# The first stage's step behind the next sequence's value product, in two groups of heads

## The chip, the cores and the metric

The kernel runs on one core of one Trainium2 chip. The metric is the time of one execution on the device in microseconds (us); the time before is the median of 3 runs, 1147.43 us.

## The reference

The input x has 8 sequences of 512 tokens with 512 features, in float32. Each token is normalized; the normalized x goes into two branches, whose product is added to x:

```python
xn = _layernorm(x, axis=-1)
s = _L0_attn_ref(xn, Wq, Wk, Wv, Wo, Wg1, Wg2, norm_weight)
g = _silu(_L0_ffn_ref(xn, gate_w, Wg, Wu, Wd, sWg, sWu, sWd, shared_gate_w))
x = x + s * g
```

The first branch is attention with a decay, without softmax, in 16 heads of 32 features, computed in chunks of 128 tokens with a state that is carried from chunk to chunk:

```python
q = rotate(silu(x @ Wq)); k = rotate(silu(x @ Wk)); v = x @ Wv
scores = einsum('bthd,bshd->bhts', qi, ki) * D          # D: decay, causal
o_intra = einsum('bhts,bshd->bthd', scores, vi)
o_inter = einsum('bthd,bhde->bthe', qi * decay_q, S)
S = lam_C * S + einsum('bshd,bshe->bhde', ki * decay_k, vi)
o = group_rmsnorm(o * sigmoid(x @ Wg1 @ Wg2)) * weight
return o @ Wo
```

The second branch is a mixture of experts: a router picks 4 of 16 experts for each token, each expert is a gated two-layer network with 128 hidden features, and a shared expert with its own gate is added:

```python
probs = softmax(flat @ gate_w.T); weights, chosen = top_k(probs, 4)
out_e = (silu(flat @ Wg[e]) * (flat @ Wu[e])) @ Wd[e]
mixed = sum of weights (normalized) * out_e;  return mixed + shared * sigmoid(flat @ shared_gate_w)
```

## The kernel before

The program is written out from Python, without a loop on the device. Engines are PE (matmuls), DVE and ACT (vector work; both also read the results of PE out of PSUM), POOL, and SP, which issues most DMAs. Each engine works its own queue in order. A wait for a tile, or for a buffer that a new tile takes over, stops the engine at that instruction and all that is queued behind it. A recording layer puts each engine's instructions in an order; those of PE are held in the order of the text (`on_pe`, L211 on, ties each group to the one before), and the others follow from it.

The stages, in order of time:

- The first stage, written as the generator `first()`, goes over all 8 sequences. For each it normalizes x (`norm`), transposes it on PE (`turn`, L277 on: 16 transposes into PSUM tiles psT, L289, copied by ACT into xT, L291, stored by SP, L297), computes the router's logits (`route_1`: plT, L306; `route_2`: pl, L318, from which DVE makes lg, L320; `route_3`: DVE picks the four experts and makes the tile mask, L331 to L345), and the shared expert (`share_1`: pg and pu, L355; `share_2`: pys, L371, four products, copied by ACT into sh, L374, stored by SP, L375). Its pieces end at the `yield`s.
- Attention of sequence 0 runs beside the end of the first stage: `along()` takes, on average, 9 pieces of `first()` for every 5 of its calls. It is handed to `sequence(0, ...)` as `step`.
- `sort()`, also a generator, takes the masks of all sequences and works out where each token stands in the lists of the experts: ptotal and pbefore on PE (L387), copied by ACT (L388), then a chain on DVE and POOL (L393 to L468), and the routing weights wt (exp on ACT, L470; products on POOL, L471 and L475; den on DVE, L473 and L474).
- Attention of sequence 1, with the building of the lists (`table`, DVE and ACT, products pn, L565) between its matmuls; the experts' weights (wexp) are loaded meanwhile.
- The block stage: rows are gathered by expert (L1153, POOL) and go through the experts.
- Attention of sequences 2 to 7, each with the mixture of the experts' outputs beside it.

In `sequence(b, step, ...)` the 16 heads are taken in 4 groups of 4 (g = 0 to 3). For each group: `scores` (state products into pk, L714; the scores ps, L725, in four PSUM tiles, one for each head; DVE multiplies each with the decay into sc, L750), a `step`, then for g = 0 and 1 the key product of group g + 2 (`key`, pk, L659), and for g = 2 and 3 the value product of the next sequence, `value(n, 0)` and `value(n, 2)` (pv, L615, four matmuls of 512 columns, which the profile shows as 8; ACT copies pv into v, L619). Then `by_token` (L691), a second step, the query product or `value(n, 1)`, `output` (po, L766 and L772; on, L776), and a third step. Behind the four groups come `value(n, 3)`, `squares` (sq on ACT, L783; pr on PE, L786), `inverse` (L790, L794) and the first key and query products of the next sequence.

PSUM has eight banks: seven are given out by `bank(tag)`, four of tag "a" (ps, psT, plT, pl, two of the four pys, ptotal, pbefore, pr and others), one "m" (pk of `key`, pg, even pv, the third pys), two "d" (pq, pu, odd pv, the first pys, po), and one "k". A new tile takes the bank of its tag that the recording layer expects free first, and waits for the last reader of the tile before it.

Which pieces the two edited steps take in sequence 0: in the third group (g = 2) the one piece `turn(7)`; in the fourth (g = 3) `route_2(7)` and `share_2(7)`.

Of the kernel before, what the change touches and what calls it, by code (L numbers as in the profile page):

```python
# [22 lines left out]
G, HG = 4, 4  # L23
# [74 lines left out]
def tile_block(ctx: ExitStack, tc: tile.TileContext, a: dict, out: bass.AP):  # L98
# [8 lines left out]
    def bank(tag, name):  # L107
        return pp.tile([P, 512], F32, tag=tag, name=name, bufs={"a": 4, "k": 1, "m": 1, "d": 2}[tag])
# [101 lines left out]
    @contextmanager  # L210
    def on_pe():  # L211

        with tc.issue_after(last_pe[-1]) if last_pe else nullcontext():
            yield
        traced = nc.cur_bb.bb.instructions
        last_pe.append(next(
            i for i in reversed(traced) if i.engine == mybir.EngineType.PE))
# [377 lines left out]
    def load_xT(b, pool=None):  # L595
        xT = (pool or home(b)).tile([P, KC, N], F32, tag="xT", name=f"xT_{b}", bufs=1)
        nc.sync.dma_start(xT.rearrange("p k n -> p (k n)"), xT_d[b])
        xT_of[b] = xT
# [10 lines left out]
    def value(b, t):  # L609
        if t == 0:  # L610
            v_of[b] = att.tile([P, NC, D], F32, tag="v", name=f"v_{b}", bufs=2)
        pv = bank("d" if t % 2 else "m", f"pv_{b}_{t}")
        for k in range(KC):
            with on_pe():
                nc.tensor.matmul(  # L615
                    pv, lhsT=xT_of[b][:, k, t * P : (t + 1) * P], rhs=wv[:, k, :],
                    start=(k == 0), stop=(k == KC - 1))
            between[0]()
        nc.scalar.copy(v_of[b][:, t, :], pv)  # L619
# [4 lines left out]
    def gate_1(b):  # L624
        pg1 = bank("a", f"pg1_{b}")
        with on_pe():
            for k in range(KC):
                for t in range(NC):
                    nc.tensor.matmul(
                        pg1[t * Q : (t + 1) * Q, :P], lhsT=wg1[:, k, :],  # L630
                        rhs=xT_of[b][:, k, t * P : (t + 1) * P],
                        start=(k == 0), stop=(k == KC - 1))
        g1_of[b] = att.tile([P, P], F32, tag="tmp", name=f"g1_{b}", bufs=TMP)
        nc.scalar.copy(g1_of[b], pg1[:, :P])

    def gate_2(b, tiles=range(NC), banks="aaaa"):
        if 0 in tiles:
            on_of[b] = home(b).tile([P, G, N], F32, tag="on", name=f"on_{b}", bufs=1)
        g1 = g1_of[b]
        p2s = {t: bank(banks[t], f"p2_{b}_{t}") for t in tiles}  # L640
        with on_pe():
            for g in range(G):
                for t in tiles:
                    tq = slice(t * Q, (t + 1) * Q)
                    nc.tensor.matmul(
                        p2s[t][:, g * P : (g + 1) * P], lhsT=wg2[tq, g * P : (g + 1) * P],
                        rhs=g1[tq, :], start=True, stop=True)
        for t in tiles:
            nc.scalar.activation(
                on_of[b][:, :, t * P : (t + 1) * P],  # L650
                p2s[t].rearrange("p (g n) -> p g n", n=P), AF.Sigmoid)
        if NC - 1 in tiles:
            g1_of.pop(b)
# [24 lines left out]
    def key(b, g, ps=None):  # L678
        kT_of[g] = rotated(b, g, "k", wk, ps)

    def query(b, g):
        qT_of[g] = rotated(b, g, "q", wq)

    def by_token(b, g):

        if not kept:
            kept.append(bank("k", f"pk_{b}_{g}"))
        pk = kept[0]
        with on_pe():
            for c in range(NC - 1):  # L690
                nc.tensor.transpose(  # L691
                    pk[:, c * P : (c + 1) * P], kT_of[g][:, c * C : (c + 1) * C], ident)
        kd = scr[0].tile([P, NC - 1, HG, HD], F32, tag="kd", name=f"kd_{b}_{g}")
        by_chunk = pk[:, : (NC - 1) * P].rearrange("p (c h d) -> p c h d", c=NC - 1, d=HD)
        for j in range(HG):
            nc.scalar.activation(
                kd[:, :, j, :], by_chunk[:, :, j, :], AF.Copy,
                scale=dk[:, g * HG + j : g * HG + j + 1])
        kd_of[g] = pk[:, (NC - 1) * P :], kd
# [55 lines left out]
    def output(b, g):  # L755
        po = bank("d", f"po_{b}_{g}")
        st, qd, sc = st_of.pop(g), qd_of.pop(g), sc_of.pop(g)
        with on_pe():
            for c in range(1, NC):
                if carry:  # L760
                    nc.tensor.matmul(  # L761
                        po[:, c * C : (c + 1) * C], lhsT=st[:, c - 1, :], rhs=qd[:, c - 1, :],
                        start=(c == 1), stop=False)
                for j in range(0 if carry else HG):
                    hs = slice(j * HD, (j + 1) * HD)
                    nc.tensor.matmul(  # L766
                        po[hs, c * C : (c + 1) * C], lhsT=st[hs, c - 1, :], rhs=qd[hs, c - 1, :],
                        start=(c == 1), stop=False)
            for c in range(NC):
                for j in range(HG):  # L770
                    h = g * HG + j
                    nc.tensor.matmul(  # L772
                        po[j * HD : (j + 1) * HD, c * C : (c + 1) * C],
                        lhsT=v_of[b][:, c, h * HD : (h + 1) * HD],
                        rhs=sc[j][:, c], start=False, stop=(c == NC - 1))
        nc.vector.tensor_tensor(on_of[b][:, g, :], po, on_of[b][:, g, :], ALU.mult)  # L776
# [16 lines left out]
    def inverse(b):  # L793
        nc.vector.reciprocal(rs_of[b], rs_of[b])  # L794
# [18 lines left out]
    def project(b, t):  # L813
        pw = bank("d", f"pw_{b}_{t}")
        with on_pe():
            for g in range(G):
                nc.tensor.matmul(  # L817
                    pw, lhsT=on_of[b][:, g, t * P : (t + 1) * P], rhs=wo[:, g, :],
                    start=(g == 0), stop=(g == G - 1))
        return pw  # L820
# [36 lines left out]
    def sequence(b, step, projected, before=None, defer=False, also=lambda: None):  # L857


        n = b + 1  # L860

        def project_tiles(q, ts):
            if q is not None:
                for t in ts:
                    projected(q, t, project(q, t))


        fill = ([0], [1], [2], [3], [], [], [], [])
        for g in range(G):
            scores(b, g)  # L870
            step()
            if g + 2 < G:
                key(b, g + 2)
            else:
                value(n, 2 * (g - 2))
            if g + 1 < G:
                by_token(b, g + 1)
            project_tiles(before, fill[2 * g])
            step()
            if g + 2 < G:  # L880
                query(b, g + 2)
                if g + 3 == G and n not in xT_of:
                    load_xT(n)
            if g + 2 == G:
                value(n, 1)
            if g == 0 and b not in on_of:
                gate_2(b)
            project_tiles(before, fill[2 * g + 1])
            if fill[2 * g + 1] == [NC - 1]:
                on_of.pop(before, None)  # L890
            output(b, g)
            if defer and g + 2 == G:
                gate_1(n)
            step()
        v_of.pop(b)
        if n == FIRST:
            for _ in range(4):
                next(filling)
            gate_1(n)
            next(filling, None)  # L900
            for e in range(E - LATE // 2, E):
                nc.sync.dma_start(wexp[:, e, :], a["experts"][:, e, :])
            squares(b)
            inverse(b)
            value(n, 3)
            normed(b)
            experts_of_blocks()
            return
        if defer:
            gate_2(n)  # L910
        value(n, 3)
        also()
        squares(b)
        step()
        inverse(b)
        key(n, 0)
        also()
        query(n, 0)
        normed(b)
        also()  # L920
        if not defer:
            step()
        key(n, 1)
        by_token(n, 0)
        if defer:
            step()
        query(n, 1)
        also()
        if not defer:
            gate_1(n)  # L930
            project_tiles(b, [0, 1])
            also()
            project_tiles(b, [2, 3])
            also()
            on_of.pop(b)
        step()
# [156 lines left out]
    along()  # L1093
    enter(0, along)
    sequence(0, along, spill, also=lambda: next(sorting, None))
    for _ in sorting:
        pass
# [373 lines left out]
```

## Time and profile before

| | |
|---|---|
| runs | 1147.18, 1147.43, 1147.70 us; median 1147.43 |
| the profiled execution | 1147.87 us, its span 1146.0 us |
| mean granted clock of PE | 0.997 |
| busy over the span | PE 1114.3 us (97%), DVE 753.2 (66%), POOL 444.8 (39%), ACT 428.8 (37%) |
| scores of sequence 0's third group (ps, L725) | start at 153.13 us |
| scores of sequence 0's fourth group | start at 178.51 us |
| sorting starts on PE (ptotal, L387) | 188.79 us |
| first gather of the block stage (L1153) | 286.98 us |

PE is the bound almost everywhere: what counts is where it idles. Times in a timeline are counted from the start of the span. A row merges instructions of one kind that follow each other; `x16` is their number, and the bracket at the end has how long the engine idled before and what it waited for. "issue" means that nothing the profile shows held it. Busy times of PE include a modelled end of each matmul, so the length of a block is better read from the start of one row to the start of the next.

### The profile page before, as it was taken

To read this page: it belongs to the slowest core of one execution; us is meant where nothing else is said; L and a number is where in the kernel's file an instruction comes from. 1 tells how busy PE (TensorE), PEld (TensorE's weight loads), DVE (VectorE), ACT (ScalarE), POOL (GpSimd) and SP (SyncE) were. 2 spreads that over 40 slices of the span, in tenths; PEclk is the share of its full clock that TensorE was granted. 3 is DMA by queue.
4 is the path that set the end of the run, shared out by engine and by line. 5 is a ranking of instruction groups with operands and counts; after the bars stand their busy time and mean duration, and the time that the engine had idled before them with its cause. 6 is when DMAs were issued, how large, how long until landed. Compare 5 with 4: busy or idle time off the path is not lost. (4 is left out here: it accounts for less than half of the span.)

```text
span 1146.0 us, 21657 instructions
## 1 busy us (share of the span) xinstructions
PE 1114.3 (97%) x7838; PEld 685.4 (60%) x7838; DVE 753.2 (66%) x1608; ACT 428.8 (37%) x924; POOL 444.8 (39%) x430
## 2 busy tenths in 40 slices
PE   7999999999999999999999999999999999999998
PEld 4445554455567777777777885555645545546453
DVE  6358744998345454454555666868789497797774
ACT  3223424254353333333333442252442522522541
POOL 4213100200323333333332314835868848858111
PEclk9999999999999999999999999999999999999999
DMA  9995431191789999999999976714747528544012
GB/s 342 317 316 192 155 133 47 47 383 46 234 184 234 252 237 237 241 235 235 233 235 273 251 192 251 264 49 147 233 125 250 165 86 256 149 129 139 20 38 74
DMA packets 163932, 218.50 MB, mean 191 GB/s; under 512 B 89840, under 2 KB 99184, under 8 KB 161776
## 3 DMA queue, kind: packets, MB, share of 16 engines
q1 hardware_dynamic: 142704, 146.76, 41.5%
q0 software_dynamic: 21120, 70.34, 23.5%
q8 instruction: 64, 1.05, 0.4%
q14 instruction: 44, 0.36, 0.1%
HBM read 126.78 MB, written 72.43 MB: 174 GB/s over the span
## 5 line engine op out<-in xcount | busy, mean ns | idle before, releaser
L1222 PE MATMUL pgu<-xts,wst 128*128 128x256 f32 x896 | 202.6, 379 | 0.0
L1222 PEld LDWEIGHTS pgu<-xts,wst 128*128 128x128 f32 x896 | 170.1, 190 | 46.2 <-issue 19.9
L1321 POOL DMA_INDIRECT yg<-y_d,place x128 | 140.1, 1095 | 30.7 <-issue 19.7
L1153 POOL DMA_INDIRECT more<-xn_d,slot x69 | 65.5, 950 | 218.9 <-DVE w L1206 107.2
L1237 PE MATMUL py<-wexp,slb 128*128 x272 | 130.0, 594 | 1.5 <-DVE slb L1229 1.5
L1241 DVE TENSOR_SCALAR y<-py,w 128x512 f32<-128x512 f32 x136 | 101.9, 751 | 42.7 <-PE py L1237 23.7
L615 PE MATMUL pv<-wv,xT 128*128 128x512 f32 x256 | 118.6, 604 | 1.3 <-ACT sh L374 1.0
L659 PE MATMUL pk<-xT,wk 128*128 128x512 f32 x256 | 118.1, 603 | 0.0
L659 PE MATMUL pq<-xT,wq 128*128 128x512 f32 x256 | 115.7, 593 | 0.4 <-PEq L1285 0.4
L1228 ACT ACTIVATE slb<-pgu 128x256 f32<-128x256 f32 (+1 forms) x80 | 28.1, 351 | 214.7 <-PE pgu L1222 163.0
L1153 POOL DMA_INDIRECT xg<-xn_d,slot x67 | 63.8, 952 | 104.7 <-DVE w L1206 36.7
L817 PE MATMUL pw<-wo,on 128*128 128x512 f32 x224 | 100.5, 595 | 3.8 <-DVE m L1359 3.1
L1363 POOL TENSOR_TENSOR xo<-xo,m 128x512 f32<-128x512 f32 x31 | 45.3, 1460 | 142.1 <-DVE m L1359 134.8
L1229 DVE TENSOR_TENSOR slb<-slb,pgu 128x256 f32<-128x256 f32 (+1 forms) x80 | 30.5, 381 | 104.7 <-ACT slb L1228 60.1
L1204 DVE COPY wst<-wexp 128x512 f32 x160 | 61.3, 424 | 43.3 <-DVE y L1241 18.3
L1186 ACT COPY xts<-pl 128x512 uint16<-128x512 uint16 x110 | 84.4, 770 | 2.2 <-DMA pl<-xg 1.7
L750 DVE TENSOR_TENSOR sc<-ps,dmask 128x512 f32<-128x512 f32 x128 | 79.1, 678 | 3.6 <-remote 1.9
L659 PEld LDWEIGHTS pq<-xT,wq 128*128 128x128 f32 x256 | 47.2, 190 | 54.2 <-issue 53.3
L615 PEld LDWEIGHTS pv<-wv,xT 128*128 128x128 f32 x256 | 46.2, 191 | 52.1 <-issue 47.6
L659 PEld LDWEIGHTS pk<-xT,wk 128*128 128x128 f32 x256 | 46.2, 189 | 50.7 <-issue 48.3
L817 PEld LDWEIGHTS pw<-wo,on 128*128 128x128 f32 x224 | 41.3, 190 | 52.9 <-issue 45.2
L1237 PEld LDWEIGHTS py<-wexp,slb 128*128 128x128 f32 x272 | 45.4, 191 | 29.2 <-issue 26.8
(193 smaller groups left out, 1724.9 us busy)
## 6 DMA issues: line engine op xcount, KB each, us to landing
y_d<-y SPq DMA_DIRECT2D x136, 256.0 KB
wexp<-in_experts SPq DMA_DIRECT2D x16, 768.0 KB
sh_d<-sh SPq DMA_DIRECT2D x32, 256.0 KB
xT<-xT_d SPq DMA_DIRECT2D x8, 1024.0 KB
m<-sh_d SPq DMA_DIRECT2D x32, 256.0 KB
xo<-in_x SPq DMA_DIRECT2D x32, 256.0 KB
out<-xo SPq DMA_DIRECT2D x31, 256.0 KB
x<-in_x SPq DMA_DIRECT2D x7, 1024.0 KB
```

The costliest lines, as they stand in the source:

```text
L615: nc.tensor.matmul(pv, lhsT=xT_of[b][:, k, t * P : (t + 1) * P], rhs=wv[:, k, :], start=(k == 0), stop=(k == KC - 1))
L659: nc.tensor.matmul(ps, lhsT=w[:, k, g * P : (g + 1) * P], rhs=xT_of[b][:, k, :], start=(k == 0), stop=(k == KC - 1))
L750: masked[:] = [nc.vector.tensor_tensor(s, pss[j].rearrange("p (c t) -> p c t", t=C), dmask[:, g * HG + j].unsqueeze(1).to_broadcast([P, NC ...
L817: nc.tensor.matmul(pw, lhsT=on_of[b][:, g, t * P : (t + 1) * P], rhs=wo[:, g, :], start=(g == 0), stop=(g == G - 1))
L1153: nc.gpsimd.indirect_dma_start(out=row(i), out_offset=None, in_=xn_d, in_offset=bass.IndirectOffsetOnAxis(ap=slot[:, i : i + 1], axis=0))
L1186: (nc.vector.tensor_copy if j in by_dve else nc.scalar.copy)(xt[:, u, KP:, :].bitcast(U16).rearrange("p k (t h) -> p h k t", h=2), pls[j % ...
L1204: nc.vector.tensor_copy(to, wflat[:, bass.ds(off + u * KC * F, KC * F)])
L1222: nc.tensor.matmul(pg[:, o * n * P : (o + 1) * n * P], lhsT=wst[j % 2][k // KP][:, (k % KP * 2 + o) * F :][:, :F], rhs=xt[:, :, k, :], sta ...
L1237: nc.tensor.matmul(py, lhsT=hT[:, u * P : (u + 1) * P], rhs=wflat[:, bass.ds(off + KC * 2 * F, D)], start=True, stop=True)
L1241: gone.append(nc.vector.tensor_scalar(y, py, w[:, u : u + 1], None, ALU.mult).ins)
L1321: nc.gpsimd.indirect_dma_start(out=yg, out_offset=None, in_=y_d, in_offset=bass.IndirectOffsetOnAxis(ap=place[:, r, g : g + 1], axis=0))
L1363: nc.gpsimd.tensor_tensor(xo, xo, m, ALU.add)
```

## The change

In sequence 0 (`b == 0`), for the third and fourth group (`g + 2 >= G`), the first of the three steps of a group is taken behind the value product of sequence 1 and no longer between the scores and that product. Everything else, the other sequences and groups too, is as it was. Lines below the edit are 4 further down.

```diff
         for g in range(G):
             scores(b, g)
-            step()
+            late_step = b == 0 and g + 2 >= G
+            if not late_step:
+                step()
             if g + 2 < G:
                 key(b, g + 2)
             else:
                 value(n, 2 * (g - 2))
+            if late_step:
+                step()
             if g + 1 < G:
                 by_token(b, g + 1)
             project_tiles(before, fill[2 * g])
```

## The prediction

> **What bounds the kernel now.** I first read the page: PE is busy 97% of the span, so time is won only where PE stands still or stops coming back late. The chain of waits holds no piece between 140 and 330 us (asked for that window, it answers 0 pieces), so the edited place, sequence 0, had to be read elsewhere. Second, the waits of PE between 150 and 195 us (columns: instruction, line, what it waited for; us, times, longest):
>
> ```profile
> PE psT L289 <- DVE sc L750: 1.0, 1, 1.0
> PE pv L615 <- ACT sh L374: 1.0, 1, 1.0
> PE pl L318 <- DVE sc L750: 0.8, 1, 0.8
> ```
>
> These are all that PE waits for there, and each stands at one of the two edited places. Third, the timeline there (start us, us, engine, line, operation, tiles):
>
> ```profile
> 153.13 1.17 PE L725 MATMUL ps<-qT,kT 32*128 32x128 f32 x32
> 154.61 2.48 DVE L750 TENSOR_TENSOR sc<-ps,dmask 128x512 f32<-128x512 f32 x4
> 155.35 2.43 PE L289 MATMUL psT<-ident,x 128*128 128x128 f32 x16 [1.04 <-DVE sc L750]
> 157.61 3.60 PE L615 MATMUL pv<-wv,xT 128*128 128x512 f32 x8
> ...
> 178.51 1.17 PE L725 MATMUL ps<-qT,kT 32*128 32x128 f32 x32
> 179.70 2.49 DVE L750 TENSOR_TENSOR sc<-ps,dmask 128x512 f32<-128x512 f32 x4
> 180.44 0.33 PE L318 MATMUL pl<-ident,lT 128*128 128x128 f32 x1 [0.77 <-DVE sc L750]
> 180.61 3.60 PE L371 MATMUL pys<-sw,h 128*128 128x512 f32 x8
> 182.10 0.22 DVE L320 COPY lg<-pl 128x68 f32<-128x68 f32 x1
> 183.20 1.28 ACT L477 ACT_TABLE_LOAD   x1
> 184.53 0.48 DVE L345 TENSOR_TENSOR mask<-mask,oh 128x64 f32<-128x64 f32 x2
> 185.25 3.70 PE L615 MATMUL pv<-wv,xT 128*128 128x512 f32 x8 [1.04 <-ACT sh L374]
> 186.99 0.63 ACT L470 ACTIVATE wt<-wt 128x512 f32<-128x512 f32 x1
> 188.79 1.02 PE L387 MATMUL ptotal<-mask,ones 128*128 128x512 f32 x2
> ```
>
> The scores of a group fill all four banks of tag "a"; DVE empties them one by one in 2.48 us, and the step behind them (psT in the third group, pl and pys in the fourth) wants just those banks. In the fourth group the value product then wants the bank of tag "m" that pys has filled and that ACT empties late, behind a table load. Fourth, what follows:
>
> ```profile
> 201.00:228.00 27.00, 27.00 (x151) 12.59 (x153) 25.35 (x47) 5.05 (x14) 5.95 (x5) 1.00 0.12 32
> 228.00:287.00 59.00, 55.05 (x711) 33.26 (x715) 54.17 (x100) 30.40 (x96) 0.02 (x1) 0.94 0.58 220
> ```
>
> ```profile
> 201.41 0.01 DVE L671 LOAD_MASK_SELECT swk<-sk  x1 [2.03 <-ACT sk L669]
> ```
>
> The windows give PE, PEld, DVE, ACT, POOL, then PE's clock and the DMA share. From 201 us on DVE is nearly full (25.35 of 27, 54.17 of 59 us), so a gain of PE lasts only if DVE's stretch starts earlier too. The third fence says that it does: its first instruction has idled 2.03 us for sk, which ACT makes from a key product of PE.
>
> **The change, part by part.** Read as a plain order of instructions, the changed kernel has the same instructions; on PE the four value matmuls pv(1,0) stand ahead of psT(7), and pv(1,2) ahead of pl(7) and pys(7). On ACT their copies go along; on SP the store sg_d goes ahead of two sh_d stores; DVE and POOL keep their order.
>
> *Removed, third group.* From the start of ps to the start of psT: 155.35 - 153.13 = 2.22 us. The same ps block, with something behind it that needs no "a" bank, takes 1.10 (227.87 to 228.97, timeline). So 1.12 is wait. The psT block takes 157.61 - 155.35 = 2.26; unhindered, at 130.49 to 132.24, 1.75. So 0.51 more. Together 1.63 us. In the changed order pv needs the "m" bank, whose reader (sl, ACT, 149.48 for 0.60) is long done, and the load of xT(1): issued at 143.93, and the DMA share falls from 0.87 in 147 to 148 us to 0.36 in the next and 0.02 in the one after, so it has landed by 150, while pv would start at 153.13 + 1.10 = 154.23. Then psT starts at 154.23 + 3.44 = 157.67 (3.44 is pv's block, 157.61 to 161.05), after the last mask (154.61 + 2.48 = 157.09). No wait is left.
>
> *Removed, fourth group.* ps to pl: 180.44 - 178.51 = 1.93 against 1.10, so 0.83; pl to pys 0.17 against 0.11 (136.00 to 136.11), so 0.06; pys to pv: 185.25 - 180.61 = 4.64 against 3.44 (161.48 to 164.92), so 1.20. Together 2.09 us.
>
> *Added, fourth group.* Everything here is 1.63 earlier: ps at 176.88, pv(1,2) at 177.98 (its "m" bank was read by sl at 174.85 - 1.63), pl at 181.42, pys at 181.53, ptotal at 184.97. Three new neighbours have to be paid or covered. (a) pys(7) 2 takes pv's bank: pv is copied by ACT at about 181.6 to 182.2, that product comes at 181.53 + 2 x 0.86 = 183.25. Covered by 1.0. (b) ptotal needs the mask, and its cover shrinks from pys and pv to pys alone. Before: lg starts at 182.10 and the mask ends at 185.01, 2.91 us. Now lg starts 0.31 behind pl (161.37 to 161.68 in the third group), at 181.73, so the mask is done at 184.64. Covered by 0.33. (c) ACT has v's copy (0.58), sgs (0.2), a table load (1.28), the sigmoid (0.23), three sh copies (0.53 each), the second load (1.28) and then exp: it starts at about 186.7, hardly earlier than the 186.99 of before, and is done at 187.4. POOL's product (1.52) and DVE's den and reciprocal (0.69, 0.35) end near 190.1, and on(0,3) is queued behind them on DVE; its sq on ACT ends near 191.4. PE's pr, which waits for it, would come at 192.3. Covered by 0.9. DVE's counting of lists behind it ends at about 194.8, and kT needs it at 201.41 - 3.7 = 197.7. Covered.
>
> *Moved DMAs.* SP's store of xT(7), issued at 158.47, goes out about 2 us later; behind it wait only the sh_d stores, whose data comes at 161.6 or later. The two sh_d(7) stores behind sg_d go out near 184.4 instead of 182.28. No stage before the last reads either, some 500 us on: nothing. What is left unknown is small: (a) to (c) between nothing and, for (b), 0.5 us if the chain on DVE runs as slowly as its slowest pieces; I take nothing, by the margins.
>
> **Sum.** 1.63 + 2.09 = 3.72 us off PE. The profiled execution took 1147.87 us, 1.87 around its span of 1146.0; it would take 1144.2. The median of the runs shown is 1147.43, 0.44 below it; so 1147.43 - 3.7 = **1143.7 us**, with 1143.0 to 1144.5 as this case's own range.
>
> **Rivals.**
> 1. *The second half is eaten by the mask.* ptotal waits for DVE, as the cover of 3.44 us is only 0.33 longer than needed. For it: some twenty small operations of DVE follow each other there, with gaps that vary. Against: DVE has nothing else to do there. If all 2.09 us come back as this wait, 1147.4 - 1.6 = 1145.8.
> 2. *ACT's chain outlasts its 0.9 us.* If each of the two table loads of part (c) holds ACT as long again as its row shows (1.28), exp, den and sq come 2.6 later, pr waits 1.7, and the time is 1147.4 - 2.0 = 1145.4. Against: the load starts at 183.20 and the sigmoid behind it at 184.49, 1.29 us with everything. The Trainium skill ("ScalarE: Activation LUTs", What ACT_TABLE_LOAD costs) has about 1.38 us of drain beside a load of some 1.28, which by an estimate would leave a gain of 1.8; the trace shows no such drain here.
> 3. *DVE's full stretch takes it all.* If the lists on DVE and ACT (part c) come no earlier, PE arrives 3.7 us sooner at 228 to 287 us and waits there for DVE: 1147.4. For it: DVE at 92% there, and PE already waits for it (pn 2.6 us in two waits between 195 and 330 us). Against: the 2.03 us of idle, and 1.02 us before the reciprocal at 198.43.
> 4. *Slower: the clock.* In two places of 228 to 287 us PE idles for 1.4 us (before 239.81) and 2.3 us (before 275.67), and from about 240.4 to 244.3 and 275.6 to 278.9 its granted clock is 0.50. There po takes 1.33 and 1.94 instead of 0.86 and 1.08, pn 2.12 instead of 1.23 and pv 3.30 instead of 2.84: about 1.4 us for each stretch. After waits of 1.04 us (at 155 and 185) the clock stays 1.00. If rival 3 holds and the 3.7 us turn up there as two more waits of over 1.4 us, two more slow stretches cost 2.8: 1150.2. It decides once a single wait there grows past some 1.4 us. Against: it needs DVE not to move. The Trainium skill ("TensorE: Matmul & The Clock Gate", Part 1) has the activity windows run freely at some 3.4 us, by which even an unchanged wait can fall into a window another way; the trace agrees that the slow stretches last 3.3 to 3.9 us.
> 5. *More.* With PE 3.7 us earlier, one of the two slow stretches is missed: 1143.7 - 1.4 = 1142.3.
>
> **How the numbers follow.** Forecast 0.76, rival 1 0.05, rival 2 0.04, rival 3 0.06, rival 4 0.05, rival 5 0.04. A measurement of this kernel can tell about 0.2%, 2.3 us, from no change. Faster by more: the forecast and rival 5, 0.80. Within it: rivals 1 to 3, 0.15. Slower: rival 4, 0.05. The range 1142.3 to 1145.9 runs from rival 5 to just past rival 1 and holds 0.89; rivals 3 and 4 stay outside.
>
> **What would show it.** In the profile after, PE's waits for sc at L289 and L318 and for sh at L374 are gone between 150 and 195 us; psT takes 1.9 instead of 2.43; ptotal starts at about 185.0 instead of 188.79, pr at 192.3 instead of 196.03, the key product behind at 193.3 instead of 197.04, and the first gather on POOL near 283.3 instead of 286.98. Rival 1 shows as a wait of ptotal for the mask; rival 2 as a wait of pr for sq; rival 3 as ptotal early and the gather where it was; rival 4 as a lower clock in the window 228 to 287, now 0.94. The forecast is wrong if ptotal is early and the block stage is not.

## The result, and the profile after

The changed kernel takes 1144.17 us in the median against 1147.47 us of the kernel before, both over 20 runs on the same chip. The ratio is 0.9974 with a 95% interval of 0.9962 to 0.9986: 0.26% less, or about 3.0 us (1.6 to 4.4). The profiled execution took 1144.77 us (before: 1147.87), its span 1142.9 (1146.0), at the same mean granted clock of 0.997.

The timeline of PE in the kernel after, in the two edited groups and behind them (start us, us, engine, line, operation, tiles, count; a bracket would hold idle time):

```profile
153.05 1.17 PE L725 MATMUL ps<-qT,kT 32*128 32x128 f32 x32
154.15 3.70 PE L615 MATMUL pv<-wv,xT 128*128 128x512 f32 x8
157.69 1.91 PE L289 MATMUL psT<-ident,x 128*128 128x128 f32 x16
...
176.90 1.17 PE L725 MATMUL ps<-qT,kT 32*128 32x128 f32 x32
178.00 3.70 PE L615 MATMUL pv<-wv,xT 128*128 128x512 f32 x8
181.54 0.27 PE L318 MATMUL pl<-ident,lT 128*128 128x128 f32 x1
181.65 3.60 PE L371 MATMUL pys<-sw,h 128*128 128x512 f32 x8
185.08 1.02 PE L387 MATMUL ptotal<-mask,ones 128*128 128x512 f32 x2
...
192.32 1.08 PE L786 MATMUL pr<-sq,sel 128*32 128x128 f32 x32
```

No row has a bracket: the value product stands between the scores and the step in both groups, and the three waits that the prediction showed are gone. (The view of PE's waits from 150 to 195 us has no lines left.) The two groups no longer hold PE, so ptotal starts at 185.08 instead of 188.79 and pr at 192.32 instead of 196.03. This execution was 0.08 us ahead of the one before already at the third group's ps; that is taken off below.

The engines beside it, DVE first, then ACT, then POOL's first gather, each in the timeline of the kernel after:

```profile
181.85 0.23 DVE L320 COPY lg<-pl 128x68 f32<-128x68 f32 x1 [1.28 <-PE pl L318]
184.28 0.48 DVE L345 TENSOR_TENSOR mask<-mask,oh 128x64 f32<-128x64 f32 x2
...
189.97 0.63 DVE L776 TENSOR_TENSOR on<-po,on 128x512 f32<-128x512 f32 x1
190.51 1.82 DVE L393 TENSOR_TENSOR_SCAN incl<-reset,total 128x512 f32<-128x512 f32 x1
...
197.71 0.01 DVE L671 LOAD_MASK_SELECT swk<-sk  x1 [1.53 <-ACT sk L669]
```

```profile
182.41 1.28 ACT L477 ACT_TABLE_LOAD   x1
183.70 0.23 ACT L477 ACTIVATE sgs<-sgs 128x32 f32<-128x32 f32 x1
...
186.69 0.63 ACT L470 ACTIVATE wt<-wt 128x512 f32<-128x512 f32 x1
190.63 0.63 ACT L783 ACTIVATE sq<-on 128x512 f32<-128x512 f32 x1 [0.19 <-DVE on L776]
```

```profile
283.44 1.23 POOL L1157 DMA_INDIRECT more<-xn_d,slot  x1 [66.31 <-DVE slot L586]
```

The mask is done at 184.28 + 0.48 = 184.76, and ptotal, which reads it, starts 0.32 us later without a wait. ACT's sq ends at 190.63 + 0.63 = 191.26, 1.06 us before pr wants it. DVE begins its full stretch at 197.71 instead of 201.41, and the first gather comes at 283.44 instead of 286.98, 3.54 us earlier.

The same two windows as in the prediction (columns: us, then busy us and instructions of PE, PEld, DVE, ACT, POOL, then PE's granted clock, the DMA share, GB/s), kernel after:

```profile
201.00:228.00 27.00, 27.00 (x168) 12.99 (x163) 26.23 (x47) 7.89 (x27) 5.95 (x5) 1.00 0.25 87
228.00:287.00 59.00, 55.04 (x686) 32.74 (x684) 51.51 (x94) 27.88 (x82) 2.95 (x3) 0.94 0.58 221
```

DVE's busy time from 228 to 287 us falls from 54.17 to 51.51, because its stretch started earlier and so ends earlier in the window. PE's clock there is unchanged at 0.94.

### The profile page after: what moved, and what is told of

The parts are those of the page before. It is cut to its first block, busy times and chain, and to the rows that moved or that the text cites. A ratio compares the mean times of both kernels' runs of the same rounds, so it can differ in the third digit from the quotient of the medians.

```text
span 1142.9 us, 21658 instructions
## 1 busy us (share of the span) xinstructions
PE 1113.9 (97%) x7838; PEld 685.6 (60%) x7838; DVE 755.9 (66%) x1608; ACT 427.7 (37%) x924; POOL 444.6 (39%) x430
## 6 DMA issues: line engine op xcount, KB each, us to landing
wexp<-in_experts SPq DMA_DIRECT2D x16, 768.0 KB
```

## The experiments

All were timed in five rounds beside the kernel before. They ran on chips where the kernel before takes 1137.6 to 1139.1 us, not 1147.5 as in the first comparison, so only ratios are comparable. Most of their intervals are about as wide as the effects, so what follows rests on traces, one for each kernel: on the time from the third group's ps to ptotal (the edited place) and from ptotal to the first gather (where the gain may be given back). "Slow" counts the stretches of some 3.5 us in which PE's granted clock is near 0.5, between 228 and 287 us.

| kernel | ps to ptotal | ptotal to gather | slow | this / before, us | ratio, 95% |
|---|---|---|---|---|---|
| before | 35.66 | 98.19 | 2 | | |
| after | 32.03 | 98.36 | 2 | 1144.17 / 1147.47 | 0.9974 (0.9962–0.9986) |
| third | 34.13 | 97.84 | 1 | 1135.14 / 1138.57 | 0.9977 (0.9957–0.9997) |
| fourth | 33.56 | 98.35 | 2 | 1137.47 / 1138.57 | 0.9985 (0.9962–1.0008) |
| bank | 34.35 | 96.88 | 1 | 1138.06 / 1138.57 | 0.9994 (0.9974–1.0014) |
| gate | 32.04 | 97.44 | 1 | 1135.14 / 1138.57 | 0.9975 (0.9954–0.9996) |
| mask2 | 32.94 | 97.56 | 1 | 1135.38 / 1137.60 | 0.9982 (0.9964–1.0001) |
| mask2b | 35.65 | 97.17 | 1 | 1138.63 / 1137.60 | 0.9999 (0.9981–1.0017) |
| changed | 32.03 | 98.28 | 2 | 1136.53 / 1139.12 | 0.9970 (0.9948–0.9992) |
| all4 | 32.03 | 97.53 | 1 | 1137.82 / 1139.12 | 0.9992 (0.9972–1.0012) |
| acts | 32.03 | 101.36 | 1, long | 1140.86 / 1139.12 | 1.0012 (0.9990–1.0034) |
| acts2 | 32.03 | 99.81 | 1, long | 1135.08 / 1139.01 | 0.9961 (0.9944–0.9978) |

### Each half by itself: third, fourth

```diff
-            late_step = b == 0 and g + 2 >= G
+            late_step = b == 0 and g + 2 == G      # third
+            late_step = b == 0 and g + 1 == G      # fourth
```

> The late step in the third group alone; the fourth group as before. Theory (each group's stall is removed by its own value product): from the start of the third group's ps to the start of ptotal 35.66 - 1.53 = 34.1 us (35.66 before, 32.03 after the whole change); PE still waits 0.8 for sc at pl and 1.0 for sh at pv; the time is some 1.5 us below before. Rival (the change works as a whole, through the earlier sort): PE arrives early but the gather of the block stage stays where it was, and the time with it.

> The late step in the fourth group alone. Theory: 35.66 - 2.10 = 33.6 us from ps to ptotal; PE still waits 1.0 for sc at psT in the third group; the time is some 2.1 us below before, so that the two halves add up to the whole. Rival (the mask's cover was too thin, and only the third group's start made it fit): ptotal waits for the mask.

PE's waits from 150 to 195 us, first in the kernel "third", then in "fourth" (what waited, for what: us, times, longest):

```profile
PE pv L615 <- ACT sh L374: 1.0, 1, 1.0
PE pl L318 <- DVE sc L750: 0.8, 1, 0.8
```

```profile
PE psT L289 <- DVE sc L750: 1.0, 1, 1.0
```

Each kernel has lost just the waits of its own half. "third" brings ptotal 35.66 - 34.13 = 1.53 us closer to ps, "fourth" 2.10; the sum, 3.63, is what both together bring (35.66 - 32.03). The halves do not touch each other.

### The fourth group's two causes: bank

The old order is kept, and pv(1,2) alone takes a bank of tag "d" instead of the "m" bank that pys has filled.

```diff
-        pv = bank("d" if t % 2 else "m", f"pv_{b}_{t}")
+        pv = bank("d" if t % 2 or (b, t) == (1, 2) else "m", f"pv_{b}_{t}")
```

> The order of before, but pv(1,2) is put into a bank of tag d in place of the m bank that pys has just filled. Theory (the 1.20 us at the fourth group's value product are the m bank's, which ACT empties behind a table load; the rest is the four a banks): pv follows pys at once, ps to ptotal 35.66 - 1.2 = 34.5 us, the waits for sc (1.0 and 0.8) stay, the time is some 1.2 us below before. Rival (all of it is the a banks): no difference to before.

PE's waits from 150 to 195 us in the kernel "bank":

```profile
PE psT L289 <- DVE sc L750: 1.0, 1, 1.0
PE pl L318 <- DVE sc L750: 0.8, 1, 0.8
```

The wait of pv for ACT's copy sh is gone, the two for sc stay, and ps to ptotal shortens by 35.66 - 34.35 = 1.31 us. PE's timeline in "bank" shows of what that is made:

```profile
181.89 3.60 PE L371 MATMUL pys<-sw,h 128*128 128x512 f32 x8
185.32 3.60 PE L615 MATMUL pv<-wv,xT 128*128 128x512 f32 x8
188.76 1.02 PE L387 MATMUL ptotal<-mask,ones 128*128 128x512 f32 x2
```

pv follows pys after 3.43 us instead of 4.64, which is 1.21 less, and pv itself takes 3.44 us instead of the 3.54 that it took behind the wait. So 1.21 of the fourth group's 2.10 is the "m" bank, where the prediction had 1.20 of 2.09. The other 0.10 belongs to this order alone: in the changed kernel pv takes 3.54 again (178.00 to 181.54).

### The cover of the mask: mask2, mask2b

The small DVE operations that make the last sequence's mask are done twice, in the changed kernel (mask2) and in the kernel before (mask2b); the output is the same.

```diff
-        for q in range(TOPK):
+        for _ in range(2 if b + 1 == B else 1):
+            for q in range(TOPK):
...
```

> The changed kernel; DVE picks the experts of the last sequence's tokens twice (the same seven small operations a second time, 1.28 us). It measures the cover that ptotal has left. Theory (the cover is the four pys alone, 0.3 us longer than the chain): the mask ends at 184.76 + 1.28 = 186.04, ptotal waits about 0.96 for it, and the time is 1.0 above the changed kernel's. Rival (there is more cover than that): no wait and no difference.

> The same double picking in the kernel of before. There pys and the value product both stand between pl and ptotal, so the mask has 3.5 us more: it ends at 185.0 + 1.3 = 186.3, ptotal at 188.8 does not wait, and the time is that of before.

The mask's first and last row in the timeline of DVE and the row of ptotal in that of PE, kernel "mask2":

```profile
181.68 0.23 DVE L320 COPY lg<-pl 128x68 f32<-128x68 f32 x1 [1.28 <-PE pl L318]
...
185.19 0.48 DVE L346 TENSOR_TENSOR mask<-mask,oh 128x64 f32<-128x64 f32 x2
```

```profile
185.82 1.10 PE L388 MATMUL ptotal<-mask,ones 128*128 128x512 f32 x2 [0.74 <-DVE mask L346]
```

The repetition lengthens DVE's chain, from lg to the end of the mask, from 2.91 to 3.99 us: by 1.08, where 1.28 was expected. In the changed order ps to ptotal grows by 32.94 - 32.03 = 0.91 us; in the old order by nothing (35.65 against 35.66). So the cover, now pys alone, had 1.08 - 0.91 = 0.17 us to spare. That is less than the 0.32 between the mask and ptotal in the kernel after, because a ptotal that does wait starts 0.15 us behind the mask's end (185.67 to 185.82). A mask slower by more than 0.17 us would have made rival 1 real; with this one it did not happen.

### Does DVE limit what comes later: gate, acts, acts2

If rival 3's mechanism exists, taking away a wait of PE in the stretch where DVE is full must gain nothing. In the changed kernel PE waits there 1.4 us at p (L645), the product of sequence 1's gate, whose four tiles take all four "a" banks, one of which DVE still reads (wexp, L576). "gate" puts the fourth tile in a "d" bank:

```diff
-                gate_2(b)
+                gate_2(b, banks="aaad" if b == 1 else "aaaa")
```

> The changed kernel, with the fourth gate tile of sequence 1 (p, L645) in a bank of tag d in place of the a bank that pn has filled and DVE empties. This takes away PE's wait of 1.38 us there. If PE's order is what limits the stretch from 228 to 287 us, the time falls by 1.4 us, and by about 1.4 more if the slow clock behind the wait goes too: the first gather at 280.6 to 282 in place of 283.4. If DVE, 90% busy there, is what limits it, PE's next waits for DVE (pn, 2.3 us) grow by what was won and the gather stays at 283.4.

PE's waits in the kernel after from 195 to 330 us, as far as they lie ahead of the gather, then in "gate" from 195 to 290 us:

```profile
PE pn L565 <- DVE sc L750: 2.6, 2, 2.3
...
PE p L645 <- DVE wexp L576: 1.4, 1, 1.4
PE pw L817 <- DVE on L810: 0.8, 1, 0.8
```

```profile
PE pn L565 <- DVE sc L750: 4.0, 3, 2.3
PE pw L817 <- DVE on L810: 0.8, 1, 0.8
PE po L766 <- ACT sq L669: 0.2, 1, 0.2
```

The wait of p is gone, and the 1.4 us stand in pn's waits for DVE instead (2.6 to 4.0). ptotal to gather is 97.44 us, among the 96.88 to 97.84 of the other kernels with one slow stretch and the same code there. Against the kernel after it is 0.92 less, but one slow stretch went with the wait; against the three that have the change, one slow stretch and still a wait at p (97.53 to 97.84: "third", "mask2", "all4") it is only 0.1 to 0.4 less, of 1.4. The gather came at 282.63 us, between the two forecasts. So it is mainly DVE that sets the length of this stretch, and most of a gain of PE within it comes back as another wait.

Then it should help to take work from DVE. "acts", on top of "gate", gives ACT the multiplication of the lists by the token's number that DVE does for half of them; "acts2" does so only in the later lists.

```diff
-                if u == 0:
+                if u == 0 and i < 2 * GROUP:      # acts2; acts leaves the whole statement out
                     nc.vector.tensor_tensor(
                         place[:, us], place[:, us], rows(half_token[...]), ALU.mult)
...
-            for j in range(max(some[0], GROUP // 2), some[1]):
+            for j in range(max(some[0], GROUP // 2 if i < 2 * GROUP else 0), some[1]):   # acts2
+            for j in range(some[0], some[1]):                                            # acts
```

> The gate kernel (fourth gate tile of sequence 1 in a d bank), and DVE's eight products of place with half_token (0.42 us each, 3.4 in all) done by ACT, row by row (0.255 each, 64 rows, 16 us more for ACT, which is busy for half of that stretch). If DVE's amount of work limits 228 to 287 us, PE's waits for DVE (4.0 us in the gate kernel) fall by up to 3.4 us and the gather comes up to 3 us earlier. If the order in which DVE and ACT get to their work limits it, ACT's longer queue is what PE and DVE wait for, and nothing is won or some is lost.

> As the kernel acts, but DVE keeps its products of place with half_token for the first two of the eight rounds of the lists, so that ACT's rows no longer stand ahead of the copies of so and of the gate's sigmoids, behind which PE waited 2.7 and 1.6 us in acts. ACT takes 48 rows in place of 64. If the amount of DVE's work is the limit of 228 to 287 us and acts lost by its two new waits alone, PE's waits for DVE fall from 4.0 to about 1.5 us and the gather stands up to 2.5 us nearer to ptotal than in the gate kernel (97.4 us). If ACT's longer queue holds up silu and with it DVE, nothing is won.

PE's waits from 195 to 290 us, in "acts" and then in "acts2":

```profile
PE pw L813 <- ACT so L1029: 2.7, 1, 2.7
PE ps L721 <- ACT on L645: 1.6, 1, 1.6
PE pn L561 <- DVE sc L746: 1.4, 1, 1.4
```

```profile
PE ps L725 <- ACT on L649: 1.8, 1, 1.8
PE pn L565 <- DVE sc L750: 1.4, 1, 1.4
PE po L766 <- ACT sq L669: 1.1, 1, 1.1
```

DVE is relieved (pn waits 1.4 instead of 4.0), and ACT takes its place: it now keeps so, on and sq back, and the gather comes 3.92 ("acts") and 2.37 us ("acts2") later behind ptotal than in "gate". That is not all of the loss. In both profiles the wait of ps for ACT is followed by a slow stretch of PE of 6.8 us; six matmuls of the key product take 5.02 and 5.09 us there instead of 2.84 in "gate", and DVE itself stands idle for 3.5 and 3.6 us until PE brings the next pn. What is ACT's queue and what the clock, these runs don't separate. Both forecasts of a gain failed. "acts2" has the lowest ratio of all, 0.9961, but its interval overlaps that of "changed" (0.9948 to 0.9992), and its profile, taken of the slowest of its twelve runs (1140.03 us, median 1135.08), gives no reason for a gain. Whether it beats the change stays open; no version was shown to.

### The change on another chip, and in all four groups: changed, all4

"changed" is the changed kernel again; "all4" takes the step late in the first two groups too, behind the key product.

```diff
-            late_step = b == 0 and g + 2 >= G
+            late_step = b == 0                     # all4
```

> The changed kernel itself, on the chip of the runs beside it, as the measure for them. If what was won before 190 us depends on PE alone, its stages start as early on every chip: ps to ptotal 32.0 us, ptotal to the first gather 97 to 98.4 us by the number of slow stretches of PE's clock that fall into 228 to 287 us (none, one or two).

> The late step in all four groups of sequence 0, the key product taking the value product's part in the first two. Theory (the step pays only where its first product wants an a bank right behind the scores; in the first two groups it is the shared expert's pg, which takes the m bank, and PE waits for nothing there): nothing won before 150 us, and as the key product and pg now want the m bank one right behind the other, the second waits for ACT to empty it, up to 1 us in each group. Rival (a product behind the scores helps in any group): the third group's ps starts earlier than 153.05 us.

"changed" repeats the local numbers to 0.1 us at a ratio of 0.9970. "all4" loses 5.00 us in its trace: from the first group's ps to the third's it takes 61.27 us (96.59 to 157.86), the kernel after 56.27 (96.78 to 153.05). (Its ratio can't show that, as its interval overlaps that of "changed".) Its timelines of PE and ACT:

```profile
102.44 3.70 PE L355 MATMUL pg<-xT,sw 128*128 128x512 f32 x8 [0.75 <-ACT sk L669]
...
124.26 3.70 PE L659 MATMUL pk<-xT,wk 128*128 128x512 f32 x8
...
129.99 5.40 PE L355 MATMUL pg<-xT,sw 128*128 128x512 f32 x8 [2.02 <-ACT sk L669]
```

```profile
128.04 1.28 ACT L669 ACT_TABLE_LOAD   x1 [4.92 <-PE pk L659]
129.34 0.60 ACT L669 ACTIVATE sk<-pk 128x512 f32<-128x512 f32 x1
```

In these two groups the product that is put ahead fills the "m" bank, and pg, the step's first product, wants that same bank and waits for ACT to empty it; the second time the copy stands behind a table load. The windows then show PE's clock (third column from the end) at 0.62 and 0.53:

```profile
130.00:132.00 2.00, 2.00 (x3) 0.95 (x4) 1.97 (x4) 0.00 (x0) 0.00 (x0) 0.62 0.00 0
132.00:134.00 2.00, 2.00 (x4) 0.73 (x3) 0.59 (x1) 0.00 (x0) 0.00 (x0) 0.53 0.00 0
```

and that pg takes 5.40 us instead of 3.70. Waits and the slow product make 0.75 + 2.02 + 1.70 = 4.47 of the 5.00 us. The expectation had up to 1 us for each wait and no clock. The move pays in the groups where the product ahead and the step use different banks.

## Why the prediction was right

**The bound and the waits.** The three waits were all that stood in the way; without them the PE marks came where the prediction put them: ptotal at 185.08 (said 185.0), pr at 192.32 (192.3), the key product at 193.33 (193.3), the first gather at 283.44 (283.3).

**The third group.** Predicted 1.63 us, measured 1.53. The term that was off is the value product's length: 3.44 us was read from a place where it stands behind the transposes psT (128*128 in the rows), but behind the scores (32*128) it takes 157.69 - 154.15 = 3.54. The psT row itself has 1.91, as said.

**The fourth group.** Predicted 2.09, measured 2.10, of it 1.21 the "m" bank (said 1.20) by the run "bank" and the rest, 0.89, the sc wait (said 0.89). Here the value product's 3.54 costs nothing new, as it took that in the old order too (185.25 to 188.79).

**The margins.** (a) held: pys shows no wait. (b): the mask was done 0.32 us before ptotal (said 0.33), but by "mask2" only 0.17 of it was cover; the prediction left out the 0.15 us from the end of the mask to a ptotal that waits for it. It held by less than it said. (c) was 1.06 (said 0.9): exp starts at 186.69 (said 186.7), and the one table load between v's copy and the sigmoid takes 183.70 - 182.41 = 1.29 us with everything. The drain of about 1.38 us that the Trainium skill adds to a load ("ScalarE: Activation LUTs", What ACT_TABLE_LOAD costs) isn't seen here either, and rival 2 did not happen. That margin was read from the trace only; no run took it away.

**Rival 3: the mechanism is there, its condition is not.** "gate" shows that from 228 to 287 us DVE mainly sets the pace and most of what PE gains there is lost again. The change's gain passes, and in the trace DVE's stretch starts 3.70 us earlier too, as the idle time ahead of kT let the prediction say.

**Rivals 4 and 5: the clock.** No new wait came up, and the kernel after has two slow stretches as the one before. That it kept both was luck: five of the nine profiles below have only one, so 0.04 was little for rival 5. Nor does a wait past 1.4 us decide, as rival 4 had it (see the last section). And their price was mis-sized. The prediction summed longer blocks to 1.4 us for each; with one stretch less ptotal to gather is 96.88 to 97.84 us (third, bank, mask2, mask2b, all4), with two it is 98.19 to 98.36 (before, after, fourth, changed). The means, 97.40 and 98.30, are 0.9 us apart.

**From 3.6 local us to the whole.** ptotal comes 3.63 us earlier, the gather 3.46 (133.85 to 130.39 from ps on), the span is 3.1 shorter, the medians 3.3 apart and the ratio says 3.0 (1.6 to 4.4). What is missing lies in code that the change doesn't touch: the block stage, from its first pt to the first key product behind it, took 387.30 us in this profile and 386.38 in the one before, and 384.57 to 389.93 over the experiments; the tail behind it took 0.48 less. With that scatter a median of 1144.17 against a forecast of 1143.7 can't be split further.

## What to carry to other kernels

When a set of results fills all buffers of one kind, put behind it on PE a product that lives in another bank, and only then the work that wants the emptied buffers; but first list which bank each of the two takes, as the same move cost 5.0 us where they shared one. A gain ahead of a stretch that another engine fills is kept only if that engine starts earlier too, so look for idle time just ahead of that stretch. And re-measure each cover that shrinks: here one of 3.4 us was left with 0.17 to spare.

## What the runs showed of the hardware

**The clock falls after short waits, and not always.** PE's wait of 1.38 us for DVE's wexp (L576) is there in both of the kernels below. The rows are PE's timeline and the windows behind it, first in the kernel after, then in "third":

```profile
236.10 1.15 PE L645 MATMUL p<-g,wg 32*128 32x128 f32 x24 [1.38 <-DVE wexp L576]
```

```profile
238.00:240.00 2.00, 2.00 (x48) 1.74 (x48) 2.00 (x4) 2.00 (x8) 0.00 (x0) 0.50 1.03 427
240.00:242.00 2.00, 2.00 (x61) 1.81 (x54) 1.97 (x7) 1.98 (x6) 0.00 (x0) 0.71 1.01 418
```

```profile
237.75 1.15 PE L645 MATMUL p<-g,wg 32*128 32x128 f32 x24 [1.37 <-DVE wexp L576]
```

```profile
238.00:240.00 2.00, 2.00 (x64) 1.68 (x64) 1.67 (x5) 1.97 (x3) 0.00 (x0) 1.00 1.02 424
240.00:242.00 2.00, 1.99 (x66) 1.63 (x58) 2.00 (x4) 2.00 (x6) 0.00 (x0) 1.00 1.03 427
```

The same wait is followed by a clock of 0.50 in one and by 1.00 in the other. The Trainium skill ("TensorE: Matmul & The Clock Gate", Part 1) ties a lower clock to an idle activity window of about 3.4 us, on windows that run freely. The traces agree with the windows more closely than the prediction's 3.3 to 3.9 us: read in windows of 1 us, each slow stretch has 3.4 us (6.8 in "acts" and "acts2"), and in one execution they start whole multiples of 3.413 us apart, such as 34.1 us (10) from 241.14 to 275.26 in the kernel before and 768.0 us (225) from 240.88 to 1008.88 in "fourth".

No idle window is needed, though: waits of 1.4 to 2.3 us were enough at times. With all twelve profiles cut on such a grid, from 60 to 1120 us, each window at full clock in which PE was busy for at most 1.56 of 3.41 us is followed by a slow one, none with more than 2.05 is, and from 1.67 to 2.05 both occur. So the place of a wait can decide. The wait for the next pn, in the kernel before and in "bank":

```profile
275.67 2.12 PE L565 MATMUL pn<-wexp 128*64 128x286 f16 x16 [2.31 <-DVE sc L750]
```

```profile
275.66 1.24 PE L565 MATMUL pn<-wexp 128*64 128x286 f16 x16 [2.31 <-DVE sc L750]
```

In the kernel before, 1.9 us of it fall into the window from 271.86 to 275.27, which leaves PE busy for 1.50, and the clock falls to 0.50. In "bank" a window ends at 274.71, in the middle of the wait; PE is busy for 2.06 and 2.47 in the two, and the clock stays at 1.00. The wait for wexp lies in one window in both kernels above (busy 2.03 and 2.05), so there the place doesn't explain the difference, which stays open.

**DVE beside POOL.** DVE's scan (L393), 1.21 us in the kernel before, took 1.82 in the kernel after, where it falls beside POOL's product of the routing weights (L475, 190.20 us for 1.06). It cost PE nothing, as DVE still idled 1.53 us for sk behind it. In all twelve profiles it takes 1.82 where the two overlap (eight) and 1.21 or 1.22 where they don't (four). No run moved POOL's product alone.
